# The output blocks' roots on GpSimd as a power of minus one half, and gathers issued one per product of R

## The chip, the cores and the metric

The kernel runs on one core of a Trainium2 chip. A time is the device time of one execution in microseconds (us). The engines are named as in the profile: PE is TensorE (PEld its weight loads), DVE is VectorE, ACT is ScalarE, POOL is GpSimd and SP is SyncE.

## The reference

Two graph layers work on 2708 nodes with 256 features. Layer 0 makes `x1 = layernorm(x + relu([x, adj x] W + b))`. Layer 1 does two steps of a dense attention that keeps, in each row, only the largest probabilities up to a mass of 0.9, and beside it two products with the normalised adjacency matrix R. Cut to what matters here:

```python
R = S + eye(N); R = R / R.sum(-1)          # S is adj: some 8 neighbours a row
for n in range(2):
    A = top_p(softmax(q(Xa) @ k(Xa).T), 0.9)
    Xf = R @ Xf
    Xa = A @ Xa
    Z = Z + Xf @ U1[n].T + Xa @ U2[n].T
h = X + Z
y = (h - mean(h)) / sqrt(var(h) + 1e-5) * ln_g + ln_b     # first root of a block
x = layernorm(X + y)                                      # second root of a block
```

All is in float32. Each output row so goes through two layer norms, that is through two reciprocal roots.

## The kernel before

The rows are cut into 22 blocks of 128 (the last, EDGE, has 20). The kernel makes layer 0 block by block, then step 1 of the attention, and then step 2, which is where the change lies. `tc.manual_schedule()` keeps the order of the work as it is written: every engine takes its instructions from its own queue in that order, and semaphores are put in where data need them. No planner moves anything.

**The periods.** Step 2 is a pipeline over the blocks, written out as a loop over `per` (L1227), with six parts `g` in each period. In a period one block gets its logits and exponentials (`exps2`, L822: ACT, Exp), the next one tries for its threshold on ACT (`try_act`, L932: Relu and Sign over the whole row), the one before gets its exact threshold on DVE (`vector_slots`, L1081), and the block of two periods ago is multiplied: `turn` (L519) transposes four tiles on PE and copies them on ACT (L528), `products` (L551) multiplies them (L562). DVE's part has six slots, one for each `g`. Slot 1 holds `below_level` (L994), one instruction over the whole row of 2720, and slot 5 ends with `mask` (L1059), another such instruction, which the transposes of that block wait for.

**The products of R.** R has few entries per row, so for each block of rows only the up to 7 x 128 columns in use are taken: their entries lie packed in `adjc_d`, and the rows of the other factor are gathered. `y_load` (L694) gathers them from `yf_d` in pass `s = 0` and from `v_d` in pass `s = 1`, with seven indirect DMAs of POOL (L698), 128 rows of 1 KB each, into one of the two halves of `yg`. `r_units(n)` (L717) issues the next n products (L728): eight for a block of rows, seven with gathered rows and one with the block's own rows, which SP loads (L714). When a block's first product is issued, `r_load` of the block after it is issued just ahead, with all of its gathers. A gather waits until the product that read the same part of `yg` two blocks before is done. Pass 0 fills the periods 0 to 9 and pass 1 the periods 11 to 21, with sixteen products, two blocks, in each period: 2, 3, 3, 2, 3 and 3 in the six parts.

**The finals.** When a block of rows has both of its sums (`arrive`, L764), its two layer norms are made by the class `Final` (L1122), two blocks at a time, over several periods. `final_slot(i)` (L1178) is called in part i, after DVE's slot:

- part 2 loads a new block's `x1 + b` (`load`);
- part 3 takes mean and variance on DVE (`stats`, L1136 and L1137, into `mvs`), of the two new blocks (first norm) and of the two that had their first norm a period ago (second norm);
- part 5 makes the roots of all four (`roots`, L1172) with one activation of ACT, 128x4;
- part 0 of the next period calls `over` (DVE: reciprocal, L1175, and the product with minus the mean, L1176), then `end` for the older blocks and `middle` for the newer ones. Both normalise on ACT (L1146) with what `over` left; `middle` then multiplies by `ln_g` and adds `x1 + b` on POOL (L1161 and L1162);
- part 1 stores the finished blocks.

DVE reaches L1176 just before slot 1, thus just before L994. After the loop over the periods three more roots follow (L1306, L1310, L1320), with the normalisations on DVE.

ACT holds one table of functions at a time. Sqrt and Exp lie in different tables, so the program contains an ACT_TABLE_LOAD ahead of a root that follows an Exp, and another ahead of the next Exp. Relu, Sign, Copy and Identity run with either.

Of the kernel before, what the change touches and what calls it, by code (L numbers as in the profile page):

```python
# [9 lines left out]
FP = mybir.dt.float32  # L10
I32 = mybir.dt.int32
AF = mybir.ActivationFunctionType
ALU = mybir.AluOpType
# [5 lines left out]
LN_EPS = 1e-5  # L19

P = 128
# [19 lines left out]
CW, CC = 128, 7  # L41
# [11 lines left out]
def gnn_two_layer_kernel(ctx: ExitStack, tc: tile.TileContext, N, xT_d, x_d, adj_d, w0_d, b0_d,  # L53
# [71 lines left out]
    with fast:  # L125
        fast_path(fast, tc, c, flags, fint, xT_d, x_d, w0_d, b0_d, w1_d, w2_d, w3_d, u1_d, u2_d, g_d, b_d)
# [22 lines left out]
def fast_path(ctx, tc, c, flags, fint, xT_d, x_d, w0_d, b0_d, w1_d, w2_d, w3_d, u1_d, u2_d, g_d, b_d):  # L149
    nc = tc.nc  # L150
# [9 lines left out]
    small = ctx.enter_context(tc.tile_pool(name="small", bufs=4))  # L160
# [14 lines left out]
    def ps_misc():  # L175
        return ps.tile([P, CH], FP, tag="misc", name="misc")
# [31 lines left out]
    for u, u_d in ((c.u1, u1_d), (c.u2, u2_d)):  # L208
        for s in range(2):
            weights.append(lambda u=u, u_d=u_d, s=s: nc.scalar.dma_start(  # L210
                out=u[:, :, s, :], in_=u_d[s].rearrange("(c p) e -> p c e", p=P)))
# [65 lines left out]
    ix = small.tile([P, NB, CC], I32, tag="ix", name="ix", bufs=1)  # L277
# [108 lines left out]
    for t in range(NB):  # L386
        p = rows(t)
# [57 lines left out]
    for m in range(NB):  # L445
        p = rows(m)
# [34 lines left out]
        if m >= ML:  # L481
            i = m - ML
# [5 lines left out]
    yg = y_room[:, :YW].rearrange("p (s c d) -> p s c d", s=2, d=D)  # L488
# [198 lines left out]
    r_queue = [(s, m) for s in range(2) for m in range(NB)]  # L687
    r_now = []
    r_in, a_in, y_in = {}, {}, {}
    arrived, loads, held = {}, {}, {}  # L690
    later = [[], []]
    ready = []

    def y_load(s, m):  # L694
        y = yg[:, m % 2]
        rows_d = (c.yf_d, c.v_d)[s].rearrange("p k d -> (p k) d")
        for i in range(CC):
            nc.gpsimd.indirect_dma_start(out=y[:CW, i, :], out_offset=None, in_=rows_d,  # L698
                                         in_offset=bass.IndirectOffsetOnAxis(ap=ix[:CW, m, i:i + 1], axis=0))
        y_in[s, m] = y  # L700

    def a_load(m):
        a = adjp.tile([P, KH, P], FP, tag="adj", name="adj_t")
        nc.sync.dma_start(out=a[:CW, :CC, :].rearrange("p c i -> p (c i)"), in_=c.adjc_d[m])
        nc.sync.dma_start(out=a[:rows(m), CC, :], in_=c.own_d[m, :rows(m), :])
        a_in[m] = a

    def r_load(s, m):
        if m not in a_in:
            a_load(m)  # L710
        if (s, m) not in y_in:
            y_load(s, m)
        y = y_in.pop((s, m))
        nc.sync.dma_start(out=y[:rows(m), CC, :], in_=(c.yf_d, c.v_d)[s][:rows(m), m, :])  # L714
        r_in[s, m] = a_in.pop(m), y

    def r_units(n):  # L717
        for _ in range(n):
            s, m = r_queue[0]
            p = rows(m)  # L720
            if not r_now:
                r_now[:] = [ps_misc(), 0]
                if m + 1 < NB:
                    r_load(s, m + 1)
            acc, k = r_now
            a, y = r_in[s, m]
            kw = CW if k < CC else p
            nc.tensor.matmul(acc[:p, :D], lhsT=a[:kw, k, :p], rhs=y[:kw, k, :], start=k == 0, stop=k == CC)  # L728
            r_now[1] += 1
            if k == CC:  # L730
                r_now.clear()
                r_queue.pop(0)
                r_in.pop((s, m))
                base = za_load(m) if s else v_load(m)
                later[1].append(lambda s=s, m=m, acc=acc, base=base: r_out(s, m, acc, base))

    def v_load(m):
        base = work.tile([P, D], FP, tag="in", name="base", bufs=3)
        nc.sync.dma_start(out=base[:rows(m)], in_=c.v_d[:rows(m), m, :])
        return base  # L740

    def za_load(m):


        if loads.get(m):
            loads[m] = 2
            return None
        loads[m] = 1
        base = work.tile([P, D], FP, tag="in", name="base", bufs=3)
        nc.sync.dma_start(out=base[:rows(m)], in_=za_d[m * P:m * P + rows(m), :])  # L750
        return base

    def r_out(s, m, acc, base):
        p = rows(m)
        if s == 0:
            nc.vector.scalar_tensor_tensor(base[:p], acc[:p, :D], rinv[:p, m:m + 1], base[:p],
                                           op0=ALU.mult, op1=ALU.add)
            nc.sync.dma_start(out=c.v_d[:p, m, :], in_=base[:p])
            if m == NB - 1:
                r_load(1, 0)  # L760
        else:
            arrive(m, base, acc, rinv[:p, m:m + 1])
# [112 lines left out]
    for t in range(NB):  # L875
        acc = ps_acc(t)
        part = exps1(t + 2) if t + 2 < NB else None
        b = None
        if t >= NB - 3:
            b = blocks[t - (NB - 3)] = Block(t - (NB - 3))  # L880
        ra_next = finish1(t + 1) if t + 1 < NB else None
        for g in range(NG):
# [26 lines left out]
            if (t, g) in y_at:  # L909
                name_y()  # L910
                y_load(0, y_at[t, g])
# [6 lines left out]
        ra = ra_next  # L918
    assert not stores and not staged and not to_turn
    r_load(0, 0)  # L920
    for f in ends:
        f()
# [194 lines left out]
    mvs = small.tile([P, 8, 2], FP, tag="mvs", name="mvs", bufs=1)  # L1117
    sds = small.tile([P, 8], FP, tag="sds", name="sds", bufs=1)
    nbs = small.tile([P, 8], FP, tag="nbs", name="nbs", bufs=1)
    nc.gpsimd.memset(mvs, 1.0)  # L1120

    class Final:  # L1122

# [45 lines left out]
            nc.sync.dma_start(out=out_d[t * P:t * P + p, :], in_=self.h[:p])  # L1169

    def roots(a, b):
        nc.scalar.activation(sds[:, a:b], mvs[:, a:b, 1], AF.Sqrt, bias=c.eps, scale=1.0)  # L1172

    def over(a, b):
        nc.vector.reciprocal(sds[:, a:b], sds[:, a:b])  # L1175
        nc.vector.scalar_tensor_tensor(nbs[:, a:b], mvs[:, a:b, 0], -1.0, sds[:, a:b], op0=ALU.mult, op1=ALU.mult)  # L1176

    def final_slot(i):  # L1178


        if i == 2:
            while ready and len(new) < 2:
                new.append(Final(*ready.pop(0)))
                new[-1].load()
        if i == 1:
            while done:
                done.pop().store()
        n = len(new) + len(finals)
        if i == 3:
            for k, f in enumerate(new + finals):  # L1190
                f.stats(k)
        if i == 5 and n:
            roots(0, n)
        if i == 0 and n:
            over(0, n)
            for f in finals:
                f.end()
            for f in new:
                f.middle()
            done[:] = finals  # L1200
            finals[:] = new
            new.clear()
# [12 lines left out]
    for b in (b0, b1, b2):  # L1215
        exps2(b, 2, *logits(1, b.t, 2))
        r_units(3)
        if b is b2:
            try_dve(b0, 1)
        run_all(begin_search(b))  # L1220
        if b is b0:
            try_dve(b0, 0)
    lg = logits(1, 3, 0)
    r_units(first - 9)
    try_act(b0, 1, 0)
    next_level(b0, 1)
    for per in range(NB + 2):  # L1227
# [11 lines left out]
        for g in range(NG):  # L1239
# [3 lines left out]
            if g == 0:  # L1243
                if b_exp:
                    shift(b_exp, lg[0])
                r_units(n)
# [36 lines left out]
    for f in later[0] + later[1]:  # L1283
# [10 lines left out]
                                   op0=ALU.mult, op1=ALU.is_lt)  # L1294
# [9 lines left out]
    n = len(new) + len(finals)  # L1304
    last.stats(n)
    roots(0, n + 1)  # L1306
    over(0, n + 1)
    last.middle()
    last.stats(5)
    roots(5, 6)  # L1310
    for f in finals:
        f.end()
        f.store()
    for k, f in enumerate(new):
        f.middle()
        f.stats(6 + k)
    over(5, 6)
    last.end()
    last.store()
# [366 lines left out]
```

## Time and profile before

| | |
|---|---|
| median of 3 runs | 1333.98 us (1332.23 to 1335.18) |
| the profiled execution | 1335.27 us, span 1333.5 us |
| busy in the span: PE, DVE, ACT, POOL | 1245.0, 1001.6, 754.5, 639.1 us |
| step 2 with finals, 1093.1 to 1226.4 us (133.3 us, five periods): PE, DVE, ACT, POOL busy | 120.1, 121.3, 124.3, 105.3 us |
| roots on ACT (L1172) | 14, of 0.29 to 0.30 us, 1065.9 to 1325.2 us |
| table loads on ACT from 1064 us on | 15, of 1.283 us: 8 at L1172, 7 at L823 |
| gathers of `yg` on POOL (L698) | 308, 0.94 to 3.7 us each, landing 3.8 us after issue (median; 2.7 to 6.3) |
| "middle" on POOL (L1161, L1162) | 19 of each, 0.72 to 0.82 us |

The profile is of one execution. Its times run from the start of its span, and the end of a span and the time of the execution differ by the 1.8 us that lie around it. A wait is shown with the instruction that ended it. [...]

### The profile page before, as it was taken

The numbers are of one execution on the slowest core, as the hardware profiler recorded it, in microseconds if no ns is written. First come the engines' busy times: TensorE is split into PE (matmuls) and PEld (weight loads), VectorE is DVE, ScalarE is ACT, GpSimd is POOL, SyncE is SP. The second block draws the span as 40 slices with busy tenths as digits, with TensorE's granted clock in tenths as the row PEclk, the third lists the DMA queues.
The fourth block names the chain that finished last, engine by engine and source line by source line (L and its number), as shares of the span: only waits on it lengthen the run. The fifth ranks groups of instructions, "written<-read, shape, count | busy, mean of one in ns | idle before, by whom it ended". The sixth has DMA issues, their size and how long they took to land.

```text
span 1333.5 us, 18733 instructions
## 1 busy us (share of the span) xinstructions
PE 1245.0 (93%) x5676; PEld 880.6 (66%) x5676; DVE 1001.6 (75%) x3420; ACT 754.5 (57%) x1348; POOL 639.1 (48%) x594
## 2 busy tenths in 40 slices
PE   8999999979899999999999868999999989998985
PEld 6877878833476666766676436777766766665764
DVE  2445555875898887877771378989898899899996
ACT  1010111025465565565655468888888899989931
POOL 1000000004375432677556278888727767778850
PEclk9999999989899999999999879999999999999998
DMA  7455554514222220233224265555625445644541
GB/s 190 158 176 166 166 160 147 168 56 124 87 76 81 66 63 10 62 92 96 74 67 106 88 181 170 176 176 160 196 52 169 153 126 155 186 149 143 159 117 38
DMA packets 101993, 166.26 MB, mean 125 GB/s; under 512 B 17394, under 2 KB 74358, under 8 KB 101882
## 3 DMA queue, kind: packets, MB, share of 16 engines
q1 hardware_dynamic: 75596, 108.91, 25.4%
q0 software_dynamic: 20544, 51.17, 14.4%
q10 hardware_dynamic: 5742, 4.89, 1.3%
q8 instruction: 47, 0.77, 0.2%
q14 instruction: 64, 0.52, 0.1%
HBM read 130.87 MB, written 34.03 MB: 124 GB/s over the span
## 4 chain that ended last, share of the span: by engine, by line
PE 71%; ACT 14%; DVE 11%; issue 3%; DMA 1%; POOL 0%; ACTq 0%; DVEq 0%
PE acc L562 24%; PE acc L255 15%; PE lg L505 8%; PE tr L525 6%; PE misc L728 5%; PE misc L677 3%; ACT e L937 3%; ACT e L823 3%; PE acc L649 2%; DVE e L1059 2%; ACT e L940 2%; PE acc L460 2%; PE misc L424 2%; PE misc L390 2%; ACT wT L528 2%
## 5 line engine op out<-in xcount | busy, mean ns | idle before, releaser
L528 ACT COPY wT<-tr 128x512 f32<-128x512 f32 (+2 forms) x258 | 132.1, 519 | 204.6 <-PE tr L525 201.9
L562 PE MATMUL acc<-ya,wT 128*128 128x256 f32 (+1 forms) x924 | 234.9, 394 | 11.5 <-ACT wT L528 11.0
L562 PE MATMUL acc<-x,wT 128*128 128x256 f32 (+1 forms) x924 | 230.5, 388 | 0.0
L698 POOL DMA_INDIRECT yg<-v_d,ix x154 | 194.9, 1265 | 73.7 <-PE lg L505 27.1
L698 POOL DMA_INDIRECT yg<-yf_d,ix x154 | 193.5, 1257 | 71.5 <-PE misc L728 35.3
L562 PEld LDWEIGHTS acc<-x,wT 128*128 128x128 f32 (+1 forms) x924 | 165.2, 189 | 79.5 <-issue 46.9
L562 PEld LDWEIGHTS acc<-ya,wT 128*128 128x128 f32 (+1 forms) x924 | 170.9, 194 | 66.6 <-ACT wT L528 22.9
L255 PE MATMUL acc<-y,adj_t 128*128 128x257 f32 (+1 forms) x924 | 208.4, 382 | 0.0
L728 PE MATMUL misc<-yg,adj_t 128*128 128x256 f32 (+1 forms) x704 | 185.1, 398 | 12.6 <-DMA yg<-yf_d,ix 6.9
L255 PEld LDWEIGHTS acc<-y,adj_t 128*128 128x128 f32 (+1 forms) x924 | 171.8, 189 | 32.7 <-issue 8.9
L365 POOL DMA_INDIRECT adj_t<-in_adj,ix x154 | 163.2, 1060 | 51.5 <-issue 40.9
L505 PE MATMUL lg<-k,q 64*128 64x512 f32 (+3 forms) x528 | 152.1, 604 | 26.8 <-ACT e L827 22.4
L728 PEld LDWEIGHTS misc<-yg,adj_t 128*128 128x128 f32 (+1 forms) x704 | 126.5, 193 | 64.8 <-issue 17.0
L525 PE MATMUL tr<-ident,e 128*128 128x128 f32 (+2 forms) x946 | 147.8, 275 | 3.5 <-DVE e L1059 3.5
L525 PEld LDWEIGHTS tr<-ident,e 128*128 128x128 f32 (+2 forms) x946 | 114.0, 140 | 43.3 <-issue 19.8
L332 POOL DMA_DIRECT2D part_d<-e x1 | 0.6, 573 | 286.1 <-DVE e L331 286.1
L568 DVE MAX8 cand<-e 128x8 f32<-128x170 f32 (+1 forms) x352 | 87.5, 318 | 36.6 <-ACT e L512 36.6
L437 ACT COPY x1T<-tr 128x256 f32<-128x256 f32 (+1 forms) x22 | 8.0, 364 | 186.6 <-PE tr L436 186.6
L937 ACT ACTIVATE e<-e,st 128x2708 f32<-128x2708 f32 (+1 forms) x43 | 113.5, 2640 | 0.1
L940 ACT ACTIVATE e<-e,st 128x2708 f32<-128x2708 f32 (+1 forms) x42 | 110.9, 2642 | 0.1
L1001 DVE MAX8 cand<-w 128x8 f32<-128x136 f32 (+1 forms) x440 | 106.9, 285 | 0.0
L505 PEld LDWEIGHTS lg<-k,q 64*128 64x128 f32 (+1 forms) x528 | 39.3, 183 | 61.7 <-ACT e L827 30.1
(233 smaller groups left out, 1775.6 us busy)
## 6 DMA issues: line engine op xcount, KB each, us to landing
adj_t<-in_adj SPq DMA_DIRECT2D x44, 704.0 KB
adj_t<-adjc_d SPq DMA_DIRECT2D x44, 448.0 KB
adjc_d<-adj_t SPq DMA_DIRECT2D x22, 256.0 KB
base<-za_d SPq DMA_DIRECT2D x41, 128.0 KB
adjc_d<-adj_t SPq DMA_DIRECT2D x22, 192.0 KB
xt<-in_x ACTq DMA_DIRECT2D x21, 128.0 KB
x_d<-x SPq DMA_DIRECT2D x21, 128.0 KB
x1b_d<-xb SPq DMA_DIRECT2D x21, 128.0 KB
```

The source lines that it names most:

```text
L255: nc.tensor.matmul(acc[:p, :n], lhsT=halves[k // KH][:kw, k % KH, :p], rhs=y[:kw, k, :n], start=k == 0, stop=stop and k == NB - 1)
L365: nc.gpsimd.indirect_dma_start(out=a[:CW, i, :], out_offset=None, in_=adj_rows, in_offset=bass.IndirectOffsetOnAxis(ap=ix[:CW, m, i:i + 1] ...
L505: nc.tensor.matmul(lg[:p, h, :b - a], lhsT=q[o, t * P:t * P + p], rhs=keys[s][o, i, :b - a], start=True, stop=True)
L525: nc.tensor.transpose(tr[:kw, k % 4, :p], e[:p, k * P:k * P + kw], ident[:p, :p])
L528: nc.scalar.copy(wT[:, :full, :p], tr[:, :full, :p])
L562: nc.tensor.matmul(acc[:p, :D], lhsT=wT[:kw, k % 4, :p], rhs=y[:kw, k, :], start=k == 0, stop=k == NB - 1)
L568: nc.vector.max(dst[:p, i * 8:(i + 1) * 8], src[:p, i * step:i * step + w])
L698: nc.gpsimd.indirect_dma_start(out=y[:CW, i, :], out_offset=None, in_=rows_d, in_offset=bass.IndirectOffsetOnAxis(ap=ix[:CW, m, i:i + 1], ...
L728: nc.tensor.matmul(acc[:p, :D], lhsT=a[:kw, k, :p], rhs=y[:kw, k, :], start=k == 0, stop=k == CC)
L937: nc.scalar.activation(scr[:b.p, :N], e, AF.Relu, bias=b.nz, scale=b.l[k], accum_out=b.relu)
L940: nc.scalar.activation(scr[:b.p, :N], e, AF.Sign, bias=b.nz, scale=b.l[k], accum_out=b.sign)
L1001: nc.vector.max(b.cand[:p, 8 * i:8 * i + 8], low[:p, SEG2 * i:SEG2 * (i + 1)])
```

## The change

It has two parts. The gathers of a block's rows are no longer issued in one go: `r_load` puts their numbers into a list (`coming`), and `r_units` issues one of them ahead of each product, so that the seven of block m + 1 stand ahead of the first seven products of block m. The gathers of block 0 of each pass, and those of the first two blocks of pass 0 at the end of step 1, are issued as before. And the roots are made on POOL, with an addition and a power with exponent minus one half, so that DVE's reciprocal and ACT's Sqrt go. Who calls `roots` and `over`, and when, stays.

```diff
+    coming = []
...
+    def y_gather(s, m, i):
+        rows_d = (c.yf_d, c.v_d)[s].rearrange("p k d -> (p k) d")
+        nc.gpsimd.indirect_dma_start(out=yg[:CW, m % 2, i, :], out_offset=None, in_=rows_d,
+                                     in_offset=bass.IndirectOffsetOnAxis(ap=ix[:CW, m, i:i + 1], axis=0))
+
     def y_load(s, m):
-        y = yg[:, m % 2]
-        rows_d = (c.yf_d, c.v_d)[s].rearrange("p k d -> (p k) d")
         for i in range(CC):
-            nc.gpsimd.indirect_dma_start(out=y[:CW, i, :], out_offset=None, in_=rows_d,
-                                         in_offset=bass.IndirectOffsetOnAxis(ap=ix[:CW, m, i:i + 1], axis=0))
-        y_in[s, m] = y
+            y_gather(s, m, i)
+        y_in[s, m] = True
...
     def r_load(s, m):
         if m not in a_in:
             a_load(m)
-        if (s, m) not in y_in:
+        if (s, m) in y_in:
+            y_in.pop((s, m))
+        elif m:
+            coming.extend((s, m, i) for i in range(CC))
+        else:
             y_load(s, m)
-        y = y_in.pop((s, m))
+            y_in.pop((s, m))
+        y = yg[:, m % 2]
         nc.sync.dma_start(out=y[:rows(m), CC, :], in_=(c.yf_d, c.v_d)[s][:rows(m), m, :])
...
                 if m + 1 < NB:
                     r_load(s, m + 1)
+            if coming:
+                y_gather(*coming.pop(0))
             acc, k = r_now
...
     nc.gpsimd.memset(mvs, 1.0)
+    power = small.tile([P, 8], FP, tag="power", name="power", bufs=1)
+    nc.gpsimd.memset(power, -0.5)
...
     def roots(a, b):
-        nc.scalar.activation(sds[:, a:b], mvs[:, a:b, 1], AF.Sqrt, bias=c.eps, scale=1.0)
+        nc.gpsimd.tensor_scalar(sds[:, a:b], mvs[:, a:b, 1], LN_EPS, None, op0=ALU.add)
+        nc.gpsimd.tensor_tensor(sds[:, a:b], sds[:, a:b], power[:, a:b], op=ALU.pow)

     def over(a, b):
-        nc.vector.reciprocal(sds[:, a:b], sds[:, a:b])
         nc.vector.scalar_tensor_tensor(nbs[:, a:b], mvs[:, a:b, 0], -1.0, sds[:, a:b], op0=ALU.mult, op1=ALU.mult)
```

## The prediction

> **What bounds the kernel now.** The root that the change touches (L1172) runs only in step 2, so I first asked for that line: 14 activations of 0.29 to 0.30 us between 1065.9 and 1325.2 us, and 8 table loads. Everything before 1065 us knows no root. The start times of DVE's L1176 then give the periods: 25.7 us for the first with finals (1067.41 to 1093.11), 26.65 for the next five (133.24 / 5), 26.41, and 23.50 for the last full one (1252.76 to 1276.26). The stretch from 1093.1 to 1226.4, five like periods, has PE busy for 120.1 us, DVE 121.3, ACT 124.3 and POOL 105.3 of 133.3: nothing has 10% to spare but POOL, and POOL less than it seems, as below.
>
> In the timeline of ACT at a period's change, with start, duration, line, and idle time before it with its releaser in brackets:
>
> ```profile
> 1223.32 0.25 ACT L531 COPY wT<-tr 20x128 f32<-20x128 f32 x1
> 1223.59 1.28 ACT L1172 ACT_TABLE_LOAD   x1
> 1224.88 0.30 ACT L1172 ACTIVATE sds<-mvs,eps 128x4 f32<-128x4 f32 x1
> 1226.70 0.59 ACT L528 COPY wT<-tr 128x512 f32<-128x512 f32 x1 [1.52 <-PE tr L525]
> 1227.29 1.28 ACT L823 ACT_TABLE_LOAD   x1
> ```
>
> Two loads a period, one to bring Sqrt's table and one to bring Exp's back. They are not worth the same. After the root ACT still waits 1.52 us for PE's transposes, so the first load and the root lie inside a wait. The second delays L823 and all that follows. And DVE waits for that same line, each period:
>
> ```profile
> DVE bulk L831 <- ACT e L823: 10.6, 5, 2.1
> PE lg L505 <- ACT e L827: 8.6, 5, 1.7
> POOL yg L1161 <- ACT yg L1146: 6.6, 5, 1.3
> ```
>
> (waits of those five periods: total, times, longest). So ACT's order closes a loop with PE and sets the 26.65 us. DVE has 2.13 us of slack, POOL 1.3. POOL's timeline shows how little that is:
>
> ```profile
> 1208.74 0.73 POOL L1161 TENSOR_TENSOR yg<-yg,gb 128x256 f32<-128x256 f32 x1 [1.32 <-ACT yg L1146]
> ...
> 1211.91 0.99 POOL L698 DMA_INDIRECT yg<-v_d,ix  x1
> 1213.21 0.95 POOL L698 DMA_INDIRECT yg<-v_d,ix  x1 [0.30 <-PE lg L505]
> ...
> 1220.72 3.37 POOL L698 DMA_INDIRECT yg<-v_d,ix  x1 [0.30 <-PE tr L525]
> ```
>
> A gather takes 0.95 us and the next starts 0.30 later whatever is named as its releaser. Two a period take 3.4 us: those that start while DVE's L994 or L1059 runs, both of 3.04 us with two inputs in SBUF; each ends 0.82 us after DVE's instruction.
>
> **The Trainium skill.** *ScalarE: Activation LUTs*, What ACT_TABLE_LOAD costs: about 1283 ns for a load whatever the set, besides a drain. The trace has 15 loads of 1.283 us (8 at L1172, 7 at L823). *GPSIMD Engine Reference*, Key points: POOL shares its SBUF interfaces with VectorE and suffers from DVE instructions with two SBUF inputs; the stretched gathers agree. *GPSIMD Engine Reference*, Performance pitfalls for Q7 kernels: a chain of dependent fp32 steps costs 4 cycles a step, used below for the power, which no run here shows yet.
>
> **The change part by part.**
>
> *Moved gathers.* Of 308 gathers of yg, 287 are now issued one per product instead of seven at a block's start. Their order on POOL does not change, and each still waits only for the product eight before it. Up to the end of the period at 1067 us POOL's queue holds nothing else between them, so this costs and gains nothing. SP's loads of the block's own rows stay put. From the first period with finals on, two things stand in the queue: the four tensor operations of "middle" (L1161, L1162) had seven gathers of the half period ahead of them and now have two; the other five come behind. They stay hidden as long as they land in time. A gather issued after "middle" begins about 7 us after L1176 and lands 3.8 us after issue (the median): 12 us. Its product comes at about 17.6 us (1217.31 against 1199.71). Without that 5 us of cover PE would wait.
>
> *Removed from ACT.* 15 loads and 14 roots. Per period only Exp's load counts: 26.65 - 1.28 = 25.36 us for the loop of ACT and PE. DVE loses the reciprocal, 0.19 us from start to start: 26.64 - 2.13 - 0.19 = 24.3 us of its own.
>
> *Added to POOL, and a new wait.* Add and power stand behind all 14 gathers of a period, and DVE's L1176 waits for them. Behind L1176 on DVE's queue stand L994, the candidates, the marks and the mask L1059, for which PE's transposes wait; ACT's normalisations (L1146) wait for its result, and everything behind them on ACT. So POOL, on which DVE never waited, now closes a loop: power, two gathers, middle (which waits for ACT), twelve gathers, add, power. Its length:
>
> - Two gathers. L994 now starts just as POOL goes on. A gather that started 0.07 us before a long DVE instruction (757.54 against 757.61) took 0.95, one that started 0.21 after (827.02 against 826.81) was stretched to 3.66. If the first escapes, the second ends at 0.15 + 3.04 + 0.82 = 4.0 us; if the first is caught, it ends there and the second costs 1.3 more: 5.3. The trace can't decide; I take 4.65.
> - Middle: 1208.74 to 1211.91, 3.17 us.
> - Twelve gathers: 12 x 1.255 less the last gap of 0.30, plus 2.43 for the one stretched by L1059 (1220.72 to 1224.40 against 1.25): 17.20.
> - Add: near L356's small integer operation, 0.26 when undisturbed; 0.20, and 0.08 to the next.
> - Power of 128x4. Below: it costs what an elementwise operation does. The rows 20x128 (0.45) and 128x256 (0.73) give 0.17 + 0.0022 per column, so 0.18. By the skill's 4 cycles per dependent step, a logarithm, product and exponential of some 60 steps (my assumption) take 240 cycles, 0.2 us at the 1.2 GHz of that page, per column: 0.17 + 0.8 = 1.0. Above: if a core took its 16 partitions one by one, 0.17 + 16 x 0.8 = 13. I take 1.0.
>
> The sum is 4.65 + 3.17 + 17.20 + 0.28 + 1.0 = 26.30 us, over the 25.36 of ACT and PE and the 24.3 of DVE. So POOL becomes the bound, at nearly the old length.
>
> *The path.* In the first period with finals POOL was idle for 7.84 us before middle, so roots are in time there; middle starts at 1075.50 - 1.28 = 1074.22 and the next roots are done 3.17 + 17.20 + 1.28 later: 1095.87. Seven rounds of 26.30 bring them to 1279.97, L1176 to 1280.0, where it was at 1276.26: +3.8 us. Here it hurts that the last full period took 23.5 us, bound by DVE, while POOL needs its 26.3. From 1276.3 to 1319.9 the chain is DVE's up to the mask at 1296.8, then PE's; no root of POOL is late there (its queue has only seven gathers left), so the shift is carried. At the end three roots follow one another. The first took 0.56 us from L1137 to L1176 (1321.02 to 1321.58); now 0.35 + 1.0: +0.8. The second is covered by 1.8 us of other finals. The third: 1325.18 + 1.35 = 1326.53 against 1325.97: +0.6. In all 3.8 + 1.4 = +5.1 us. On the profiled execution's own 1335.27 (span 1333.5) that is 1340.4; the median of the runs, 1333.98, lies 1.3 lower, so I predict 1339.1.
>
> **The rivals.** *Faster: POOL keeps up.* If the power takes 0.6 us or less and the first gather escapes L994, POOL's round is 4.0 + 3.17 + 17.20 + 0.28 + 0.6 = 25.25, under the 25.36 of ACT and PE. Then six periods to the one at 1226 gain 1.28 each (7.7), and the last two, which POOL holds at 25.25 against 26.41 and 23.50, give most of it back: L1176 at 1272.9 instead of 1276.26, -3.4, and +0.6 in the tail: 1331.2; with 0.3 us, 1330.3. For it: POOL's small operations are quick. Against: all of the slack has to hold at once. It decides below a power of about 0.7 us.
>
> *Slower by far: the power goes partition by partition.* At 13 us the round is 38.3 us: the first roots are done at 1107.9, the eighth 268 later, so L1176 comes 100 us late and the tail adds some 25: about 1459. At 3 us the round is 28.3, L1176 20 us late and the tail 5 longer: 1358. Nothing in the profile speaks for or against it; that the other operations of POOL go by whole columns is against the worst.
>
> *No difference.* The loads cost nothing because another engine was as late. Against it are the waits for L823 and L827, which a load delays directly. By balance it can be, and then the time is 1331 to 1337: with the 4.65 above and a power of 0.5 us the round is 25.8, L1176 comes at 1276.0 and the tail adds 0.4, which makes 1334; with the first gather never caught, a power of 0.9 gives 1333.5.
>
> **How the numbers follow.** Anything within 0.2%, 2.7 us, can't be told from no change. Forecast (POOL's round between 26.1 and 27.3 us, 1337 to 1348) 0.46; power of several us 0.12; no difference 0.17; faster 0.25. Slower is 0.46 + 0.12 = 0.58. The range leaves out the far tail above 1350 (about 0.11) and gains beyond 1330 (about 0.06): 1330 to 1350. The forecast's own range is 1337 to 1348.
>
> **What would show it.** Right: no load left at L1172 and L823; L831's wait for L823 gone; a new wait of DVE's L1176 for POOL's power, 1 to 3 us in each period from 1095 on; POOL without idle time from 1075 to 1280; periods of 26 us also where there were 23.5. Wrong: L1176 waits for nothing (POOL keeps up), a power far from 1 us, a gather at L994 not stretched or two, products that wait for gathers, or a long first power. The weakest terms are the power and the gather at L994.

## The result, and the profile after

The changed kernel took 1345.59 us (median of 4 runs, 1344.98 to 1348.84), the kernel before 1334.58 beside it: a ratio of 1.0096, 95% interval 1.0072 to 1.0121. (Ratios here and below are taken over the single runs; the quotient of two medians can differ from them, here 1.008.) By the medians it is slower by 11.0 us, where 5.1 were predicted. The profiled execution took 1348.84 us with a span of 1347.1.

Some ten lines have been added ahead of the periods, so L1176 of before is L1188 now, L1172 has become the pair L1184 and L1185, the gathers L698 are L697, the products L728 are L738, `middle` is L1173 and L1174, ACT's normalisation L1158, L994 and L1059 are L1004 and L1069, and L823 and L831 are L833 and L841.

The starts of L1188 give the periods that L1176 gave before. They were 25.70, 26.65 five times, 26.41 and 23.50 us. They are 28.65, 27.84, 26.97, 32.10, 25.40, 29.22, 26.59 and 25.08: none is like its neighbour. L1188 of the last full period comes at 1287.23 instead of 1276.26 (+10.97), and from there to the last one it takes 51.78 instead of 49.71 (+2.07); together +13.0 us between the two profiled executions. (The profiled execution of after is the slowest of its four.)

The group of the new power, all 14, with the least, the median and the longest in ns:

```profile
L1185 POOL TENSOR_TENSOR sds<-sds,power x14: 572/1044/1052, 1054.7 to 1338.4; 128x4 f32<-128x4 f32 x8, 128x2 f32<-128x2 f32 x2, 128x3 f32<-128x3 f32 x2, 128x1 f32<-128x1 f32 x2
```

So 1.04 us for 128x4 was near the 1.0 taken. The table loads are gone: ACT has 1319 instructions instead of 1348 (15 loads and 14 roots fewer) and is busy for 730.7 us instead of 754.5. Now the waits from 1080 us to the end (total, times, longest), of before and then of after:

```profile
ACT wT L528 <- PE tr L525: 37.5, 17, 7.4
POOL yg L1161 <- ACT yg L1146: 21.1, 7, 13.2
...
DVE bulk L831 <- ACT e L823: 14.5, 7, 2.1
...
PEld misc L728 <- DMA yg<-v_d,ix: 0.7, 1, 0.7
...
PE misc L728 <- DMA yg<-v_d,ix: 0.2, 1, 0.2
```

```profile
ACT wT L528 <- PE tr L525: 66.4, 19, 6.4
DVE nbs L1188 <- POOL sds L1185: 25.5, 9, 5.5
PEld misc L738 <- DMA yg<-v_d,ix: 24.8, 19, 2.7
POOL yg L1173 <- ACT yg L1158: 21.8, 6, 9.8
...
PE misc L738 <- DMA yg<-v_d,ix: 17.6, 15, 2.3
...
DVE bulk L841 <- ACT e L833: 4.2, 3, 2.1
```

The forecast wait of L1188 for the power is there, and L841's wait for the exponential has shrunk from 14.5 to 4.2 us. But there is a line that the forecast didn't have: PE's products of R wait for gathered rows, 17.6 us in 15 places, where there were 0.2. ACT then waits 29 us longer for PE.

One period of POOL shows how (start, duration, line, idle time before it and its releaser):

```profile
1120.80 1.04 POOL L1185 TENSOR_TENSOR sds<-sds,power 128x4 f32<-128x4 f32 x1
1122.03 1.08 POOL L697 DMA_INDIRECT yg<-v_d,ix  x1 [0.19 <-PE misc L738]
1123.42 2.47 POOL L697 DMA_INDIRECT yg<-v_d,ix  x1 [0.31 <-issue]
1126.77 0.72 POOL L1173 TENSOR_TENSOR yg<-yg,gb 128x256 f32<-128x256 f32 x1 [0.87 <-ACT yg L1158]
...
1129.94 0.99 POOL L697 DMA_INDIRECT yg<-v_d,ix  x1
1131.24 0.95 POOL L697 DMA_INDIRECT yg<-v_d,ix  x1 [0.30 <-PE lg L505]
1132.49 0.95 POOL L697 DMA_INDIRECT yg<-v_d,ix  x1 [0.30 <-PE misc L738]
```

and PE's products in the same stretch (x4 is four records, two products):

```profile
1131.11 1.13 PE L738 MATMUL misc<-yg,adj_t 128*128 128x256 f32 x4
1135.34 0.60 PE L738 MATMUL misc<-yg,adj_t 128*128 128x256 f32 x2
1136.58 0.70 PE L738 MATMUL misc<-yg,adj_t 128*128 128x256 f32 x2 [0.65 <-DMA yg<-v_d,ix]
1139.54 1.22 PE L738 MATMUL misc<-yg,adj_t 128*128 128x256 f32 x2 [2.26 <-DMA yg<-v_d,ix]
```

The three products from 1135.34 on are those of part 4. They read the rows of gathers 2, 3 and 4 of their block (counted from 0), the first three behind `middle`, started at 1129.94, 1131.24 and 1132.49. The 0.95 us that such a line shows is POOL's part alone; the rows of these three landed 4.6, 5.3 and 7.0 us after it began. The first product starts 5.4 us after its gather and doesn't wait; the second waits 0.65 us for its rows and the third another 2.26. Before, part 4 was one line, without a wait:

```profile
1217.31 1.46 PE L728 MATMUL misc<-yg,adj_t 128*128 128x256 f32 x6
```

### The profile page after: what moved, and what is told of

The parts are those of the page before. It is cut to its first block, busy times and chain, and to the rows that moved or that the text cites. A ratio compares the mean times of both kernels' runs of the same rounds, so it can differ in the third digit from the quotient of the medians.

```text
span 1347.1 us, 18714 instructions
## 1 busy us (share of the span) xinstructions
PE 1253.5 (93%) x5676; PEld 883.2 (66%) x5676; DVE 994.9 (74%) x3406; ACT 730.7 (54%) x1319; POOL 647.2 (48%) x623
## 3 DMA queue, kind: packets, MB, share of 16 engines
q0 software_dynamic: 20544, 51.17, 13.5%
## 4 chain that ended last, share of the span: by engine, by line
PE 76%; ACT 9%; DVE 5%; DMA 4%; issue 3%; POOL 2%; POOLq 0%; ACTq 0%; DVEq 0%
PE acc L562 26%; PE acc L255 15%; PE lg L505 9%; PE misc L738 8%; PE tr L525 6%; DMA yg<-v_d,ix 3%; PE misc L677 3%; PE acc L649 2%; ACT e L833 2%; ACT e L837 2%; PE acc L460 2%; PE misc L424 2%; PE misc L390 2%; ACT wT L528 1%; POOL yg L697 1%
## 5 line engine op out<-in xcount | busy, mean ns | idle before, releaser
L562 PE MATMUL acc<-ya,wT 128*128 128x256 f32 (+1 forms) x924 | 236.3, 396 | 10.7 <-ACT wT L528 10.6
L562 PE MATMUL acc<-x,wT 128*128 128x256 f32 (+1 forms) x924 | 230.5, 388 | 0.0
L697 POOL DMA_INDIRECT yg<-yf_d,ix x154 | 192.7, 1251 | 71.5 <-PE misc L738 35.6
L697 POOL DMA_INDIRECT yg<-v_d,ix x154 | 186.2, 1209 | 72.7 <-DMA v_d<-base 25.0
L738 PE MATMUL misc<-yg,adj_t 128*128 128x256 f32 (+1 forms) x704 | 191.6, 404 | 29.3 <-DMA yg<-v_d,ix 17.6
L562 PEld LDWEIGHTS acc<-x,wT 128*128 128x128 f32 (+1 forms) x924 | 165.2, 189 | 79.6 <-issue 46.9
L562 PEld LDWEIGHTS acc<-ya,wT 128*128 128x128 f32 (+1 forms) x924 | 173.1, 195 | 64.2 <-issue 22.4
L738 PEld LDWEIGHTS misc<-yg,adj_t 128*128 128x128 f32 (+1 forms) x704 | 125.9, 194 | 87.1 <-DMA yg<-v_d,ix 24.8
L833 ACT ACTIVATE e<-lg,nmax 128x1024 f32<-128x1024 f32 (+2 forms) x66 | 67.0, 1016 | 14.5 <-PE lg L505 14.5
```

Source lines behind the costliest of these rows:

```text
L562: nc.tensor.matmul(acc[:p, :D], lhsT=wT[:kw, k % 4, :p], rhs=y[:kw, k, :], start=k == 0, stop=k == NB - 1)
L697: nc.gpsimd.indirect_dma_start(out=yg[:CW, m % 2, i, :], out_offset=None, in_=rows_d, in_offset=bass.IndirectOffsetOnAxis(ap=ix[:CW, m, i: ...
L833: nc.scalar.activation(e2(b.t)[:b.p, a:c_], lg, AF.Exp, bias=b.nmax, scale=1.0, accum_out=b.all[:b.p, i:i + 1])
```

## Experiments

Four causes can be told apart. **A**: the moved gathers are the loss. Of a half period's seven, five now stand behind `middle`, which waits for ACT; they come too late for the products of part 4. The late products delay PE, then ACT's copies and exponentials, then `middle` of the next period, and with it gathers and roots. **B**, the prediction's own: POOL's longer round, with roots that DVE waits for, is the loss, and the gathers cost nothing. **C**: the power as such. **D**: issuing one gather per product costs by itself, wherever `middle` stands. The theory in the expectations of e1 to e4 was A and B together, each with a part of the loss; A alone was a rival there and became the theory only with e9 and e10, where D is called theory B.

Runs e1 to e8 ran on two other chips, where the kernel before took 1376.7 us (e1 to e4) and 1369.7 us (e5 to e8); so ratios within a chip are compared, not times. In e9 to e11 it took 1333.98 us. The times in the expectations of e1 to e4 are meant for a kernel before of 1334 us.

### Each part alone: e1, e6 and e2, e7

The kernel before with the roots of the change:

```diff
...
-        nc.scalar.activation(sds[:, a:b], mvs[:, a:b, 1], AF.Sqrt, bias=c.eps, scale=1.0)
+        nc.gpsimd.tensor_scalar(sds[:, a:b], mvs[:, a:b, 1], LN_EPS, None, op0=ALU.add)
+        nc.gpsimd.tensor_tensor(sds[:, a:b], sds[:, a:b], power[:, a:b], op=ALU.pow)
...
-        nc.vector.reciprocal(sds[:, a:b], sds[:, a:b])
```

> The kernel before with the roots on POOL (add and power) and no other change: gathers again seven at a block's start. Theory (two causes: DVE's wait for roots behind POOL's gathers, and gathers that stand behind middle and come late for PE): PE's wait for gathers falls from 17.6 us to under 3, DVE still waits for the roots, 1 to 4 us a period; periods near 26.5 us; 1336 to 1341 us. Rival 1 (the roots alone are the cause): as the changed kernel, 1344 to 1347. Rival 2 (the moved gathers alone are the cause): the table loads' gain shows, 1326 to 1332.

> The roots alone, gathers as before. If the moved gathers are the whole loss and the roots alone break even (as on the chip of the first four): 0.996 to 1.002 of the kernel before, periods of about 25.3 us in place of 26.65, and the last two periods longer than the 23.5 before. If the roots on POOL cost as I forecast: 1.003 to 1.006.

Measured: e1 1375.02 us, ratio 1.0007 (0.9986 to 1.0028); e6 1366.62 us, ratio 0.9968 (0.9949 to 0.9986). In e6 the periods are 24.29, 25.27, 25.86, 25.29, 25.24, 25.25, 26.45 and 25.65 us. Beside those of the kernel before on the first chip, the first six have won 0.8 to 1.4 us each and the last has lost 2.15; from there to the last root it takes 52.89 instead of 49.71, another 3.2 lost. DVE's product with minus the mean waits for POOL's roots (8.0 us in 8 places, 4.1 of them up to the last full period), and one product of R waits 0.6 us for a gather. In e1 the periods are nearly the same (only the seventh, 25.20, differs by more than 0.1), though its ratio shows no gain. The theory of e1 had periods near 26.5 us, which missed. The roots on POOL do not make the kernel slower; the 1.003 to 1.006 that the forecast meant for them lies above both intervals.

And the changed kernel with the roots and the reciprocal of before:

```diff
...
-        nc.gpsimd.tensor_scalar(sds[:, a:b], mvs[:, a:b, 1], LN_EPS, None, op0=ALU.add)
-        nc.gpsimd.tensor_tensor(sds[:, a:b], sds[:, a:b], power[:, a:b], op=ALU.pow)
+        nc.scalar.activation(sds[:, a:b], mvs[:, a:b, 1], AF.Sqrt, bias=c.eps, scale=1.0)
...
+        nc.vector.reciprocal(sds[:, a:b], sds[:, a:b])
```

> The kernel before with the gathers moved, one per product, and the roots on ACT as before. Theory: the five gathers now behind middle land about when PE needs them, some us of waiting for gathers in the periods with finals, no wait of DVE for roots; 1334 to 1339 us. Rival 1 (roots alone): 1333 to 1336, no waits for gathers. Rival 2 (moved gathers alone): 1344 to 1347.

> The moved gathers alone, roots on ACT. If they are the loss by themselves: 1.007 to 1.014 of the kernel before, with PE waiting 10 us or more for gathers. If they cost only together with POOL's roots: 1.000 to 1.004, with under 5 us of such waits.

Measured: e2 1393.54 us, ratio 1.0140 (1.0048 to 1.0232); e7 1385.54 us, ratio 1.0107 (1.0072 to 1.0143). The gathers alone cost as much as the whole change (e5 below, on e7's chip: 1.0123), though ACT makes the roots and DVE waits for no power. The theory of e2, at most 1.004 from them, missed. PE waits 10.9 us for gathers in e2 and 9.0 in e7, whose expectation had 10 or more. In e7's profile POOL has just done `middle` (L1171, L1172 there), and the same three products of part 4 come apart:

```profile
1225.48 0.73 POOL L1171 TENSOR_TENSOR yg<-yg,gb 128x256 f32<-128x256 f32 x1 [2.57 <-ACT yg L1156]
...
1228.65 0.99 POOL L697 DMA_INDIRECT yg<-v_d,ix  x1
1229.94 0.95 POOL L697 DMA_INDIRECT yg<-v_d,ix  x1 [0.30 <-PE lg L505]
1231.19 0.95 POOL L697 DMA_INDIRECT yg<-v_d,ix  x1 [0.30 <-PE misc L738]
```

```profile
1234.05 0.60 PE L738 MATMUL misc<-yg,adj_t 128*128 128x256 f32 x2
1235.68 0.70 PE L738 MATMUL misc<-yg,adj_t 128*128 128x256 f32 x2 [1.04 <-issue]
1237.42 1.22 PE L738 MATMUL misc<-yg,adj_t 128*128 128x256 f32 x2 [1.04 <-DMA yg<-v_d,ix]
```

Again the first gather behind `middle` starts 5.4 us ahead of its product. The third product waits 1.04 us for its rows; the second is as late, with no releaser in the profile ("issue"). B falls: what it put the loss on gains or is even, and what it put at nothing is the loss.

### The place and the kind of the root: e3, e4, e5

In the changed kernel, the roots right behind the statistics in part 3:

```diff
                 f.stats(k)
-        if i == 5 and n:
-            roots(0, n)
+            if n:
+                roots(0, n)
```

> The changed kernel with the roots called in part 3, right after the statistics, so that on POOL they stand behind nine of a period's fourteen gathers instead of all. Theory: DVE's wait for the roots goes (25.5 us in nine waits now), POOL's work per period stays at some 26 us and PE still waits for gathers; 1337 to 1342. If the place of the roots is what costs, 1332 to 1336. If only POOL's work counts, as the changed kernel, 1344 to 1347.

Measured: 1392.46 us, ratio 1.0140 (1.0067 to 1.0214). DVE waits for POOL's roots in only three places any more, 2.7 us in all instead of 25.5, and nothing is gained, where the theory had 1.002 to 1.006 of the kernel before: the wait for the roots isn't what the loss comes from. PE waits 18.2 us for gathers.

A product in the place of the power, so that this kernel leaves the root out:

```diff
-        nc.gpsimd.tensor_tensor(sds[:, a:b], sds[:, a:b], power[:, a:b], op=ALU.pow)
+        nc.gpsimd.tensor_tensor(sds[:, a:b], sds[:, a:b], power[:, a:b], op=ALU.mult)
```

> The changed kernel with a multiplication in the place of the power (the scales of the final norms are left wrong): the same instructions and waits, the second of 128x4 at about 0.2 instead of 1.04 us. Theory (POOL's round is the bound, so 0.85 us times 8 rounds and twice at the end): 6 to 9 us less than the changed kernel, 1337 to 1340. If the late gathers are the bound and not the power: 0 to 3 us less, 1342 to 1346.

Measured: 1392.64 us, ratio 1.0115 (1.0029 to 1.0200), with periods as uneven as those of the changed kernel (31.36 and 26.70 side by side). The instruction takes 0.20 us instead of 1.04, and no gain is seen. The interval is wide and still reaches into what the theory had (1.002 to 1.0045), so e4 alone doesn't rule out C; what speaks against it is that e1 and e6 above, and e10 below, have the same power and aren't slower. The changed kernel itself, beside e6 to e8 on their chip:

> The changed kernel as it is, beside the others on one chip. All theories: 1.007 to 1.012 of the kernel before where the chip is like the first (1334 us before), more where gathers land later.

Measured: 1385.89 us, ratio 1.0123 (1.0094 to 1.0152); that of the result was 1.0096 (1.0072 to 1.0121).

### Only the place of middle: e9 and e10

This separates A from D. The gathers stay one per product; `middle`'s two multiply-add pairs on POOL move from part 0 to part 2, so that POOL's queue has seven gathers, `middle`, seven gathers again. ACT's normalisation stays where it was.

```diff
...
             spares.append(spares.pop(0))
             self.norm(spares[-1])
-            h = self.h
+            self.due = True
+
+        due = False
+
+        def scale(self):
+            p, h = self.p, self.h
             nc.gpsimd.tensor_tensor(h[:p], h[:p], c.gb[:p, 0, :], op=ALU.mult)
             nc.gpsimd.tensor_tensor(h[:p], h[:p], self.x1[:p], op=ALU.add)
+            self.due = False
...
         if i == 2:
+            for f in finals:
+                if f.due:
+                    f.scale()
```

e9 is this with ACT's roots (against e7), e10 with the roots on POOL (against the changed kernel).

> Moved gathers with ScalarE's roots, as in e2 and e7, but the two multiply-add pairs of middle are issued two parts later, so that POOL's queue again has seven gathers ahead of middle and seven behind it, in the very order of the kernel before. Theory A (the moved gathers cost because five of a half period's seven now stand behind middle, which waits for ScalarE): ratio to before 0.998 to 1.003, periods 25.7 to 26.7 us, products wait for gathers less than 2 us in all. Theory B (issuing one gather a product costs by itself, wherever middle stands): 1.009 to 1.014 as in e2 and e7, products go on waiting 10 us or more.

> The changed kernel (moved gathers, roots on POOL) with the same later middle: POOL's queue is then in the order of roots, seven gathers, middle, seven gathers. Theory A: the loss is gone and what is left is the roots' part alone, ratio 0.995 to 1.000 (e1 gave 1.0007, e6 0.9968), periods near 25.3 us. Theory B: 1.009 to 1.014.

Measured: e9 1333.99 us, ratio 1.0000 (0.9992 to 1.0009), periods 25.70, 26.65 five times, 26.40 and 23.49, those of the kernel before to 0.01 us. No product of R waits for a gather in it; one weight load does:

```profile
PEld misc L738 <- DMA yg<-v_d,ix: 0.2, 1, 0.2
```

e10 1329.88 us, ratio 0.9973 (0.9964 to 0.9981). Its waits from 1080 us on:

```profile
DVE nbs L1194 <- POOL sds L1191: 8.0, 8, 2.0
...
PEld misc L738 <- DMA yg<-v_d,ix: 2.9, 3, 1.5
...
PE misc L738 <- DMA yg<-v_d,ix: 1.8, 2, 1.0
```

The moved gathers cost nothing once `middle` stands behind the same seven of them; D falls, A stands. Between the changed kernel and e10 only `middle`'s place differs. The one is 11.0 us slower than the kernel before measured beside it and the other 4.1 us faster, so the place is worth some 15 us. PE's wait for gathers falls from 17.6 us to 1.8, DVE's wait for the power from 25.5 to 8.0: two thirds of that forecast wait go with `middle`'s place, though roots and power are the same.

### A better version: e8 and e11

e8 was an attempt at one: bulk gathers as before, but the last four of every second block issued behind the roots, which are made in part 3 and, in the last periods, on ACT.

```diff
...
+            if n and pool_roots:
+                roots(0, n)
+            while rest:
+                rest.pop(0)()
...
```

> Gathers seven at a time as before, but of the block that starts in part 3 the last four are issued after the roots, which are made on POOL in part 3; from the period in which the last Exp has run on (period 19) the roots are ACT's again. Then DVE waits for no root, POOL's round is 25.3 us and no longer than the loop of ACT and PE, and the last periods keep their 23.5: 1.28 us less in each of six to seven periods, 0.993 to 0.996 of the kernel before. If POOL's work itself is the bound: 0.998 to 1.003.

Measured: 1369.17 us, ratio 1.0003 (0.9985 to 1.0021): no gain, where 0.993 to 0.996 was expected. Its periods are 24.29, three of 25.25, three of some 26.45, and 24.96. POOL's round, from power to power, has no gap and takes 26.45 to 26.51 us from the first of the like periods on. The three of 25.25 are those in which POOL's delay has not yet reached the others, so without POOL the loop of ACT, PE and DVE takes 25.25 us:

```profile
1221.50 1.05 POOL L1186 TENSOR_TENSOR sds<-sds,power 128x4 f32<-128x4 f32 x1
1222.74 3.51 POOL L700 DMA_INDIRECT yg<-v_d,ix  x1 [0.19 <-PE lg L505]
...
1229.06 3.04 POOL L700 DMA_INDIRECT yg<-v_d,ix  x1 [0.30 <-issue]
```

The two gathers that DVE's long instructions catch take 3.51 and 3.04 us here.

e11 takes the gathers of before, and the roots of the change only while exponentials are still to come; afterwards ACT makes them, with one table load and none back.

```diff
...
+        pool_made.append(bool(pool_roots))
+        if pool_roots:
+            nc.gpsimd.tensor_scalar(sds[:, a:b], mvs[:, a:b, 1], LN_EPS, None, op0=ALU.add)
+            nc.gpsimd.tensor_tensor(sds[:, a:b], sds[:, a:b], power[:, a:b], op=ALU.pow)
+            return
         nc.scalar.activation(sds[:, a:b], mvs[:, a:b, 1], AF.Sqrt, bias=c.eps, scale=1.0)
...
-        nc.vector.reciprocal(sds[:, a:b], sds[:, a:b])
+        if not pool_made.pop(0):
+            nc.vector.reciprocal(sds[:, a:b], sds[:, a:b])
...
+        if per == NB - 2:
+            pool_roots.clear()
```

> Gathers as before; roots on POOL only up to the period that still has exponentials, and on ScalarE afterwards (one table load, none back). If the roots on POOL gain 1.3 us in each of the six periods to the one that ends the exponentials and lose only in the last full one and the tail: periods 24.3, 25.3, 25.3 to 25.9, 25.3, 25.3, 25.3, 26.4, 23.5 us and the tail as before, 7.7 us less than before in all, ratio 0.9935 to 0.996. If ScalarE's loop isn't what the loads held up (POOL's round takes it all): no better than e6, 0.997 to 1.000.

Measured: 1327.55 us, ratio 0.9957 (0.9944 to 0.9970), faster than both kernels. Periods 24.28, 25.26, 25.87, 25.25, 25.23, 25.26, 25.17 and 23.75. The eight sum to 200.07 us against 208.84 in e9, which has the periods of before; of the 8.8 us, 2.4 go again between the last full period and the last root (52.1 us instead of 49.7), which was expected to stay as it was. The first 1.5 of them, in the 24.8 us after the last full period (23.3 in e9), go with a wait in the profile. From 1266 to 1291 us DVE's statistics wait for `middle`, which they don't in e9 or before:

```profile
DVE bst L1139 <- POOL yg L1165: 1.7, 2, 0.9
```

POOL runs behind here: `middle` has seven gathers ahead of it after the last full period's product with minus the mean, where the kernel before has five. The other 0.9 us stay open.

## Why the prediction was right, and where it was wrong

The side was right (slower, 0.58), and the time lay in the range, 6.5 us over the forecast. The reason on record was wrong all the same: side and range were right by luck.

**The step that failed: the moved gathers.** It said that a gather behind `middle` "begins about 7 us after L1176 and lands 3.8 us after issue", that its product comes at 17.6, and so left a cover of 5 us. Three things are wrong in it, and the first two could be seen in the lines of before.

- The 7 us suppose that `middle` moves up when five gathers leave its way. But L1161 was already waiting for ACT, 1.32 us, at 1208.74. It can't start before ACT is done, so the five gathers that now follow it start where a gather after `middle` did before: at 1211.91, 12.2 us after L1176 and 5.4 ahead of the product at 1217.31. After and e7 show this 5.4 to the tenth. (Counted from L1188 the gather of after comes at 8.1 us, near the 7 forecast, but only because L1188 itself has waited 4.1 us for the power; the product comes at 13.5 then, not at 17.6.)
- One gather was priced where five were moved. The next two start 1.25 us apart, while their products follow 0.49 apart (1.46 / 3). With 5.4 us for the first, the third has 5.4 - 2 x 1.25 + 2 x 0.49 = 3.9.
- The landing of 3.8 us was a median over all gathers. Of the five that follow `middle` around 1212 us in before, the profile has the landing of one, 4.1 us. Of the five in the period of after shown above it has three, of the first, second and third gather in this order:

```profile
DMA to landing us min/median/max: 4.6/5.3/7.0
```

Already with 4.1 the cover is 1.3, then 0.5, then -0.2 us: for the last of the three it could be read off before as about nothing instead of 5 us. With the three landings of after it is 0.8, -0.7 and -3.1; measured are no wait, 0.65, and 0.65 + 2.26 = 2.9. Why the third gather took 7.0 us to land isn't settled. SP's transfers run beside it (1.87 MB from 1128 to 1141 us, the gathers 1.05), but they do so before too (1.71 and 0.92 MB from 1210 to 1223).

What isn't worked out even now is the full size: a late product holds PE, which was busy for nine tenths of a period before, and the delay comes round through ACT's copies and `middle` to the next gathers. The waits of L1173 for ACT go up and down with it (0.87 us in the period from 1122, 5.11 in that from 1149), and so do the periods. That `middle`'s place is what brings it about is shown by e9 and e10; how the delay grows from round to round is not derived.

One part of the size may lie with TensorE's granted clock. From the first to the last full period's root it stands at 0.50 for 14.0 us in after, in stretches that begin in or right after a wait for gathers, where the kernel before has 3.5 us of it, e9 none and e10 3.5. Eight multiplications of L562 take 3.62 us there (from 1140.56) instead of 1.89 (from 1147.32). Summed over the stretch, what is missing of a clock of 1.00 comes to 6.8 us in after and 1.7 in the kernel before. The six profiles with late gathers (after, e2 to e5, e7) have 7.5 to 19.5 us at this clock, the seven others 0 to 5. So it goes with the loss, but whether the waits bring it on, and how much of the 11.0 us goes through it, isn't shown: in before the one such stretch left its period at 26.65 us.

**POOL's round, 26.30 us.** This was named as the bound, with roots later than before as the loss. In e10 POOL works without a gap too, but its round takes 25.25 us, no more than the loop of ACT, PE and DVE takes by itself (e8), so which of them bounds e10 isn't shown. Its round there, from power to power:

```profile
1139.62 1.04 POOL L1191 TENSOR_TENSOR sds<-sds,power 128x4 f32<-128x4 f32 x1
1140.86 1.09 POOL L697 DMA_INDIRECT yg<-v_d,ix  x1 [0.19 <-issue]
1142.26 2.47 POOL L697 DMA_INDIRECT yg<-v_d,ix  x1 [0.31 <-PE tr L525]
...
1151.04 0.73 POOL L1178 TENSOR_TENSOR yg<-yg,gb 128x256 f32<-128x256 f32 x1
...
1160.50 2.76 POOL L697 DMA_INDIRECT yg<-v_d,ix  x1 [0.30 <-issue]
...
1164.53 0.26 POOL L1190 TENSOR_SCALAR sds<-mvs 128x4 f32<-128x4 f32 x1
1164.87 1.04 POOL L1191 TENSOR_TENSOR sds<-sds,power 128x4 f32<-128x4 f32 x1
```

Term by term, measured against taken: power 1.04 against 1.0; the two gathers at L1004 4.07 (1140.66 to 1144.73) against 4.65, the first isn't stretched; the other twelve 6.29 + 10.29 = 16.58 against 17.20, because the one that L1069 stretches takes 2.76 in this round and not 3.37; `middle` with its gap 3.19 against 3.17; from the last gather to the power 0.37 against 0.28. The sum is 25.25. So the terms were close and the slip was in the two stretched gathers, 1.2 us together; e8 shows the other case, 26.49 us with the two at 3.51 and 3.04, near the forecast's. At 25.25 the roots gain. The rival "POOL keeps up" forecast this round, from a power of 0.6, and a net gain of 2.8 us; e6 and e10 measure gains of 3.1 and 4.1 us (differences of the medians, e1 1.7), with a power of 1.04. Its threshold of 0.7 us was too low by the stretch. But its parts don't fit, only their sum: it put L1176 of the last full period 3.4 us earlier and the rest 0.6 longer, and from the first root on e6 and e10 have 5.6 and 5.7 earlier and 3.2 longer. Nor do its own words add up: gains of 7.7 less what 25.25 loses against 26.41 and 23.50 leave 7.1. The 3.4 seems to come from its chain of POOL's rounds, whose first roots are done some 2.4 us later than L1176 came before (1093.11); in e6 and e10 DVE doesn't wait for them.

**The other steps.** ACT's relief was right: its loop with PE was put at 25.36 us, and in e8 three periods in which DVE waits for no root take 25.25. The last full period loses what POOL's round exceeds DVE's 23.50 by: right, 25.65 in e6. The tail, +1.4: it measured +2.07 in the changed kernel and +3.2 in e6 and e10. In all three some 3.0 us are lost just ahead of the first of the three last roots, where 0.8 was put; DVE's wait for the power is 1.4 of these, and the rest isn't traced. The new wait of L1188 for POOL came, but not at 1 to 3 us each: it goes from nothing to 5.5 from one period to the next. "POOL without idle time from 1075 to 1280" failed: `middle` waits for ACT. "Products that wait for gathers" stood in the list of what would show the prediction wrong, and that is what the profile showed.

**How two errors met.** The loss forecast for the roots, +5.1 us, is by itself a gain of about 4 (e10), and the nothing forecast for the gathers is a loss of some 15 (after against e10). The two don't simply add: on the chip of e5 to e7 the gathers alone cost 15.9 us, the roots alone gain 3.1, and both together cost 16.2 (medians), so the roots' gain doesn't show while gathers are late. The forecast so came out on the right side by luck, for a cause that isn't there.

## What to carry to other kernels

When instructions move behind another one in an engine's queue, first ask when that one can start: if it already waits for another engine, it doesn't move up, and all that stands behind it starts as late as its releaser allows. Then price the last of the moved group, not its first, with the transfer time of that stretch and against the consumer's own pace. And a wait at a new instruction (here DVE for POOL's root) may only show a delay that began elsewhere in a loop: undo one part at a time before the wait is called the cause.

## What was not expected of the hardware

- POOL's power costs 0.57 to 0.66, 0.72, 0.89 and 1.04 us for 128 x 1, 2, 3 and 4 elements in after: about 0.46 us and 0.145 a column. The estimate (0.17 and 0.2 a column) got the sum nearly right with a smaller fixed part and a dearer column.
- A gather that starts 0.08 us after the start of a 3.10 us DVE instruction (1140.86 against 1140.78) takes 1.09 us, and one that starts 0.51 after (1222.74 against 1222.23, in e8) is stretched to 3.51. Over all the profiles kept here, every gather that starts 0.10 to 2.9 us after the start of such an instruction is stretched. Of some 80 that start within 0.09 us of it, before or after, four are stretched and the others aren't; one of the four starts 0.08 us before it (1269.26 against 1269.34 in e6, 3.93 us).
- In two places (1163.95 us in after, 1203.23 in e7) a gather behind `middle` starts 1.91 us late, with a product named as its releaser. The product that it has to wait for is that of the same place two blocks before, over 20 us back in after. What held it stays open.
- From the first to the last full period's root, TensorE's granted clock falls to 0.50 for some 3.5 to 7.5 us at a time. The six of the 13 profiles in which products wait 9 us or more for gathers have two to four such stretches, the others (3.8 us of waits at most) at most one.
